# A planner for cross-attention and RWKV: spread values as one transfer, contexts as 112 and 13 rows, eight transfers in flight

## The chip, the cores and the metric

The kernel runs on one core of a Trainium2 chip. The metric is the device time in microseconds of one execution. An execution is run several times; the median is taken. A profile is one separate execution, taken with the hardware profiler; its own time stands beside its span.

Engine names in the profile: PE is TensorE (PEld its weight loads), DVE is VectorE, ACT is ScalarE, POOL is GpSimd, SP is SyncE, which issues nearly all transfers here. A "q" behind an engine's name (SPq) is its instruction queue, in which waits and DMA issues stand. Transfers run on 16 DMA engines that all queues share.

## The reference

Two layers over 16 batches of 112 tokens, width 512, all in float32. The first is cross-attention to a context of 375 rows with 16 heads of 32; the second is an RWKV block whose recurrent state has 32 heads of 16 by 16.

```python
# layer 0
a = _layer_norm(audio_kv, ln_gamma, ln_beta)          # (16, 375, 512)
Q = (x @ Wq.T) ; K = (a @ Wk.T) ; V = (a @ Wv.T)      # 16 heads of 32
attn = softmax(Q K^T * scale)
x = x + tanh(gate) * ((attn @ V) @ Wo.T)
# layer 1
xa = _ln(x, ln1_w, ln1_b)
sx = previous token of xa - xa                        # the first one from the context
xk, xw, xv, xr, xg = xa + sx * (maa_stack + tanh((xa + sx * maa_x) @ maa_w1) @ maa_w2)
w = exp(-exp(time_decay + tanh(xw @ td_w1) @ td_w2))
r, k, v, g = xr @ Wr.T, xk @ Wk.T, xv @ Wv.T, silu(xg @ Wg.T)
def step(s, rkvw):                                    # 112 steps, 32 heads
    a = k_t[..., :, None] * v_t[..., None, :]
    out = einsum('bhi,bhij->bhj', r_t, u * a + s)
    s = a + w_t[..., :, None] * s
x1 = x + (group_norm(out) * g) @ Wo.T
xc = _ln(x1, ln2_w, ln2_b)                            # and again the token before
return x1 + sigmoid(xr2 @ Wfr.T) * (relu(xk2 @ Wfk.T) ** 2 @ Wfv.T)
```

## The kernel before

**How the work is tiled.** Tokens lie in the free dimension, features on the 128 partitions in four chunks (`NC` = 4). Two batches make a group of `N` = 224 columns (`GB` = 2), and there are eight groups (`NG` = 8). The attention runs batch by batch; the second layer runs group by group in four lanes: `front` (layer norm and mixing), `begin` and `middle` (projections and scans), `back` (gate, output projection, channel mixing). Group g's `middle` runs beside the attention of later batches.

**The scan.** The state of a head is 16 by 16. For one chunk of 128 key features (8 heads of 16, `HC` = 8, `NS` = 16) and one value column index there is one recurrence over time per partition. A step n (0 to 15 in each group; chunk c = n // 4, e = n % 4) handles four value columns q at once, in a tile `kv` of 128 x 4 x 224. For this the values, which lie one feature per partition, have to be spread: each of 8 rows goes to the 16 partitions of its head. That is done through DRAM. `values(cc)` (L1212) projects the values of two chunks and copies them from PSUM to `chk_v`; `receptances(cc)` (L1218) projects the receptances and stores `chk_v` to the DRAM tile `dram_vd` (L1222) as one transfer of 128 rows. `spread(n)` (L1261) reads `dram_vd` back into `chk_kv`, in four transfers, one for each q, each of 8 rows of 223 values, each row repeated over 16 partitions, shifted by one token (`kvs[n][:, q, 1:N]`).

Then `products(n)` (L1274) multiplies `kv` by the keys in two halves (q 0 and 1 on VectorE, q 2 and 3 on GpSimd) and writes the first column of each batch from the initial state `chk_s` (ScalarE, or GpSimd for n < 2). `scans(n)` (L1290) runs two scans on VectorE, `st = w * st + kv`, and multiplies each by the receptances on GpSimd. `summed(n)` (L1310) sums over the 16 key rows by matmuls with a constant (`keep_td1c`) on TensorE. `chk_kv` and `chk_st` have three buffers each, `chk_v` has one, `dram_vd` two.

**The contexts.** `load_context(b)` (L645) loads a batch's context, 375 rows as three blocks of 125, into `ctxp_ctx` (one buffer) with one transfer of 125 partitions x 3 x 512 values (768,000 bytes); for the first batch the block is cut into 112 and 13 rows (`T` = 112) already. `normalise(b)` (L741) takes its statistics on VectorE, TensorE transposes it (`keep_ident`), and keys and values are projected from `ctxp_aT`. The buffer is free again after the transposes.

**Weights** of the other projections are loaded in slabs of 128 x 1024 values (512 KB) into five buffers `slabs_slab`; each projection of 16 matmuls reads one slab, so that a slab load waits until TensorE has done with the slab five loads before.

**What sets the order.** The kernel body does not run on the chip directly: a `Recorder` takes down all operations with their tiles, and a `Planner` (L378) simulates them with durations for each operation (`_cost`, L263; `_transfer`, L308) and writes out the order of every engine's queue; `emit` (L561) then issues the instructions in that order, which is why nearly every line of the profile is L586. On the chip, each queue runs strictly in its order, and waits are those that the data and buffers need. In `plan` (L433) the unit that can start first is chosen, and among those of the same start the one whose `place` (its due time) is earliest. For a transfer the planner counts 430 ns of issue, the bytes' time on 16 engines and 1750 ns to land. Between operations it sees dependencies by tile; DRAM tiles count as a whole (`View.meets`, L99), so that two writes to the same DRAM tile stand one after the other in the plan.

On the chip a transfer issued by SP signals on one of eight semaphores in turn, so that a transfer waits until the eighth one before it has landed.

Of the kernel before, what the change touches and what calls it, by code (L numbers as in the profile page):

```python
# [8 lines left out]
F32 = mybir.dt.float32  # L9
# [246 lines left out]
SEM = 60.0  # L256
DRAIN, REFILL, PE_LATENCY, DMA_LATENCY = 93.0, 104.0, 165.0, 1750.0
TABLE_LOAD = 1283.0
OVERLAP = {"scalar": 105.0, "vector": 85.0, "gpsimd": 0.0}
SAME_MODE = 3.0  # L260


def _cost(op):  # L263
    n = op.writes[0].size if op.writes else 1
    psum = any(v.tile.tag.space == PSUM for v in op.reads + op.writes)
    call = op.call
    if op.engine == "vector":
        if call == "tensor_tensor_scan":
            return 55 + 2.28 * n
        if call == "tensor_tensor_reduce":  # L270
            return 60 + 1.5 * n
        if call in ("bn_stats", "tensor_reduce"):
            return 50 + 1.22 * op.reads[0].size if call == "bn_stats" else 50 + 1.9 * op.reads[0].size
        if call == "bn_aggr":
            return 170
        if call == "memset":
            return 62
        if psum:
            return 140 + 1.07 * n
        if call == "tensor_tensor":  # L280
            return 200 + 0.9 * n if n < 200 or n > 700 else 150 + 1.75 * n
        if call == "scalar_tensor_tensor":
            return 200 + 1.5 * n
        return 150 + 0.96 * n
    if op.engine == "scalar":
        t = 160 + 0.84 * n
        if isinstance(op.kwargs.get("scale"), View):
            t += 110
        if isinstance(op.kwargs.get("bias"), View):
            t += 70  # L290
        if "accum_out" in op.kwargs:
            t += 190
        return t
    if call == "tensor_tensor":
        return 880 if ALU.pow in op.args else 90 + 2.57 * n
    return 190 + 0.85 * n


PACKETS = {375: 42, 892: 45, 896: 48, 1024: 52, 2048: 101, 4096: 217, 8192: 430, 512: 35}
# [8 lines left out]
def _transfer(op):  # L308
    view = (op.writes or op.reads)[0]
    if view.tile.whole and op.reads:  # L310
        view = op.reads[0]
    size = 1 if view.tile.tag.dtype == U8 else 4
    total = (view.hi - view.lo) * view.size * size
    piece = min(_run(view.index) * size, 8192)
    if op.args[0] is not view and not isinstance(op.args[0], View):
        piece = min(piece, 896)
    packet = PACKETS.get(piece, 30 + piece * 0.05)
    return total / piece * packet / 16


def _mode(op):
# [56 lines left out]
class Planner:  # L378
# [54 lines left out]
    def plan(self):  # L433
        self.array = Array()
        self.clock = {e: 0.0 for e in ("tensor", "vector", "scalar", "gpsimd", "sync")}
        self.dma, self.table = 0.0, None
        for tag in self.recorder.tags.values():
            tag.slots = [Slot() for _ in range(min(tag.bufs, len(tag.tiles)))]
            tag.strict = tag.name not in self.LOOSE
            for tile in tag.tiles:  # L440
                tile.left, tile.last = len(tile.ops), 0.0
        waiting = {e: [] for e in self.clock}
        for u in self.all:
            u.ready = 0.0
            if not u.waiting:
                waiting[u.engine].append(u)
        todo = len(self.all)
        while todo:
            best = None
            for engine, units in waiting.items():  # L450
                pick = self.choose(engine, units)
                if pick and (best is None or pick[0] < best[0]):
                    best = pick
            if best is None:
                raise RuntimeError("the plan is stuck: " + self.stuck(waiting))
            start, unit = best
            waiting[unit.engine].remove(unit)
            self.commit(unit, start)
            for user in unit.users:
                user.waiting -= 1  # L460
                if user.waiting == 0:
                    waiting[user.engine].append(user)
            todo -= 1
# [22 lines left out]
    def choose(self, engine, units):  # L486
        found, first = [], 1e18
        for u in units:
            t = self.ready(u)
            if t is None:  # L490
                continue
            if engine == "tensor":
                start = self.array.start(u, t)
            else:
                start = max(t, self.clock[engine])
            found.append((start, u))
            first = min(first, start)
        if not found:
            return None
        best = None  # L500
        for start, u in found:
            if start > first + (DRAIN + 1 if engine == "tensor" else 0.5):
                continue
            key = self.place_of(u)
            if engine == "tensor" and u.mode == self.array.mode:
                key -= SAME_MODE
            if engine == "scalar" and self.load(u):
                key += SAME_MODE
            if best is None or (key, u.number) < best[0]:
                best = ((key, u.number), start, u)  # L510
        return best[1], best[2]
# [12 lines left out]
    def commit(self, unit, start):  # L524
        for tile in unit.holds:
            if tile.slot is None:
                tag = tile.tag
                tile.slot = self.slot(tile)
                tile.slot.tile = tile
                tag.next += 1  # L530
        engine = unit.engine
        if engine == "tensor":
            ends = self.array.run(unit, start)
            issued = self.array.end
        elif unit.ops[0].call == "dma_start":
            issued = start + 430
            begin = max(issued, self.dma)
            self.dma = begin + _transfer(unit.ops[0])
            ends = [self.dma + DMA_LATENCY]
        else:  # L540
            table = self.load(unit) if engine == "scalar" else None
            if table:
                unit.table = self.table = table
                start += TABLE_LOAD
            cost = _cost(unit.ops[0])
            ends = [start + cost]
            issued = start + max(cost - OVERLAP[engine], 45.0)
        unit.start, unit.end = start, max(ends)
        self.clock[engine] = issued
        for op, end in zip(unit.ops, ends):  # L550
            for tile in {id(v.tile): v.tile for v in op.reads + op.writes}.values():
                tile.left -= 1
                tile.last = max(tile.last, end + SEM)
                if tile.left == 0:
                    tile.slot.free_at, tile.slot.tile = tile.last, None
        for user in unit.users:
            t = issued if user.engine == engine and unit.ops[0].call != "dma_start" else unit.end + SEM
            user.ready = max(user.ready, t)
        self.order.append(unit)
# [29 lines left out]
def planned(ins, out):  # L589
# [55 lines left out]
    def load_context(b, after=None):  # L645
        raw = ctxp.tile([SC, NSC, D], F32, tag="ctx", name=f"ctx_{b}")
        rows = ins["ctx"][b].rearrange("(c p) d -> p c d", p=SC)
        if b == 0:

            for c in range(NSC):  # L650
                nc.sync.dma_start(raw[:T, c, :], rows[:T, c, :])
            nc.sync.dma_start(raw[T:, :, :], rows[T:, :, :])
            return raw
        load = nc.sync.dma_start(raw, rows)
        return raw

    def load_x(g):
# [543 lines left out]
    def parts_of(g):  # L1201
# [10 lines left out]
        def values(cc):  # L1212
            vals[cc] = duo("v", f"v_{g}_{cc}", bufs=1)
            ps = project("wv1", cc, xm[2], f"pv1_{g}_{cc}")
            nc.scalar.copy(vals[cc], ps)
            vds[cc] = dram.tile([P, 2, N], F32, tag="vd", name=f"vd_{g}_{cc}")

        def receptances(cc):  # L1218
            rs[cc] = duo("r", f"r_{g}_{cc}")
            ps = project("wr1", cc, xm[3], f"pr1_{g}_{cc}")  # L1220
            copied = nc.scalar.copy(rs[cc], ps)
            nc.sync.dma_start(vds[cc], vals[cc])  # L1222
            owns[cc] = duo("own", f"own_{g}_{cc}")
            for e in range(2):
                nc.vector.scalar_tensor_tensor(
# [35 lines left out]
        def spread(n):  # L1261

            c, e = divmod(n, NQ)
            rows = vds[c // 2][:, c % 2, :].rearrange("(q e h) t -> e h q t", q=NQ, e=NQ)[e]
            kvs[n] = chk.tile([P, NQ, N], F32, tag="kv", name=f"kv_{g}_{n}", bufs=3)
            for q in range(NQ):
                load = nc.sync.dma_start(
                    kvs[n][:, q, 1:N],  # L1270
                    rows[:, q, 0 : N - 1].unsqueeze(1).broadcast_to([HC, NS, N - 1]),
                )

        def products(n):  # L1274

# [311 lines left out]
```

## Time and profile before

| | us |
|---|---|
| median of 3 runs | 1458.59 (1455.35 to 1465.3) |
| profiled execution | 1455.53 |
| its span | 1453.8 |
| mean granted TensorE clock | 0.946 |

Transfers that the change touches, as issued by SP in the profiled execution:

| transfer | count | KB each |
|---|---|---|
| `chk_kv<-dram_vd` (spread) | 512 | 111.5 |
| `dram_vd<-chk_v` (store) | 16 | 224 |
| `ctxp_ctx<-in_ctx`, whole batch | 15 | 750 |

Issuing one spread transfer takes SP 574 ns (median). VectorE waited 84.5 us in all for spreads to land, GpSimd 203.6 us, ScalarE 196.1 us. How to read the page: the busy shares are averages over stages that differ, so what a stage is limited by is read from windows of time. Idle time of an engine is put down to what ended it. The granted clock is TensorE's, 1.0 being full speed; it falls to 0.5 for some microseconds at some places. The "chain that ended last" is followed back from the last instruction to what released each step.

### The profile page before, as it was taken

To read this page: it belongs to the slowest core of one execution; us is meant where nothing else is said; L and a number is where in the kernel's file an instruction comes from. 1 tells how busy PE (TensorE), PEld (TensorE's weight loads), DVE (VectorE), ACT (ScalarE), POOL (GpSimd) and SP (SyncE) were. 2 spreads that over 40 slices of the span, in tenths; PEclk is the share of its full clock that TensorE was granted. 3 is DMA by queue.
4 is the path that set the end of the run, shared out by engine and by line. 5 is a ranking of instruction groups with operands and counts; after the bars stand their busy time and mean duration, and the time that the engine had idled before them with its cause. 6 is when DMAs were issued, how large, how long until landed. Compare 5 with 4: busy or idle time off the path is not lost.

```text
span 1453.8 us, 23511 instructions
## 1 busy us (share of the span) xinstructions
PE 1327.5 (91%) x8484; PEld 988.1 (68%) x8484; DVE 917.6 (63%) x1743; ACT 590.7 (41%) x1480; POOL 654.6 (45%) x644
## 2 busy tenths in 40 slices
PE   8999999989989999899998999989999998878867
PEld 5656686567965679556885669747696576846646
DVE  3434647874469544794547964588448858786842
ACT  2444523453144531555235532455315535423322
POOL 3001225742447324671337633374246725595740
PEclk9999999899999999899998999989999999979868
DMA  9301035221743127421473206622174225526521
GB/s 318 114 23 52 24 116 188 80 81 39 239 155 94 53 71 256 127 74 52 125 235 111 80 30 200 205 91 83 36 240 134 82 64 184 167 92 202 157 93 50
DMA packets 115532, 174.96 MB, mean 120 GB/s; under 512 B 9864, under 2 KB 87560, under 8 KB 115160
## 3 DMA queue, kind: packets, MB, share of 16 engines
q1 hardware_dynamic: 114776, 172.83, 36.4%
q8 instruction: 67, 1.10, 0.3%
q10 hardware_dynamic: 576, 0.52, 0.1%
q14 instruction: 49, 0.40, 0.1%
q0 software_dynamic: 64, 0.10, 0.0%
HBM read 164.52 MB, written 8.91 MB: 119 GB/s over the span
## 4 chain that ended last, share of the span: by engine, by line
PE 53%; DMA 18%; DVE 12%; ACT 8%; issue 4%; SPq 3%; POOL 2%; DVEq 0%; ACTq 0%; POOLq 0%
PE ps_bank L586 53%; DMA chk_kv<-dram_vd 7%; DVE chk_st L586 4%; DMA ctxp_ctx<-in_ctx 4%; SPq L586 3%; ACT hp_pr L586 3%; DMA slabs_slab<-in_wq 3%; DVE big_x L586 2%; DMA dram_vd<-chk_v 2%; DMA slabs_slab<-in_wfr 1%; DVE chk_kv L586 1%; DVE hp_pr L586 1%; ACT tmp_tmp L586 1%; POOL chk_st L586 1%; DMA slabs_slab<-in_wg 1%
## 5 line engine op out<-in xcount | busy, mean ns | idle before, releaser
L586 POOL TENSOR_TENSOR chk_st<-chk_st,chk_r 128x448 f32<-128x448 f32 x256 | 307.2, 1222 | 168.6 <-DVE chk_st L586 156.3
L586 DVE TENSOR_TENSOR_SCAN chk_st<-ps_w_w,chk_kv 128x448 f32<-128x448 f32 x256 | 263.4, 1069 | 12.2 <-ACT ps_w_w L586 7.6
L586 POOL TENSOR_TENSOR chk_kv<-chk_kv,chk_k 128x444 f32<-128x444 f32 x128 | 155.2, 1216 | 210.2 <-DMA chk_kv<-dram_vd 203.6
L586 PE MATMUL ps_bank<-big_x,slabs_slab 128*128 128x224 f32 x1024 | 214.8, 368 | 3.1 <-DMA slabs_slab<-in_wg 2.8
L586 PEld LDWEIGHTS ps_bank<-big_x,slabs_slab 128*128 128x128 f32 x1024 | 203.1, 200 | 13.3 <-issue 6.2
L586 PE MATMUL ps_bank<-ctxp_aT,keep_wk 128*128 128x375 f32 x512 | 183.4, 507 | 3.2 <-ACT hp_prT L586 3.1
L586 DVE TENSOR_TENSOR chk_kv<-chk_kv,chk_k 128x444 f32<-128x444 f32 x128 | 125.9, 988 | 84.6 <-DMA chk_kv<-dram_vd 84.5
L586 PE MATMUL ps_bank<-keep_wv,ctxp_aT 128*125 128x512 f32 x384 | 168.6, 592 | 0.0
L586 ACT ACTIVATE hp_pr<-hp_pr,sm_mn 112x375 f32<-112x375 f32 x256 | 152.4, 598 | 31.1 <-DVE sm_mn L586 31.1
L586 DVE CUSTOM_DVE_ANT_0 hp_pr<-ps_bank,hp_mb 112x375 f32<-112x375 f32 x256 | 124.5, 541 | 43.0 <-PE ps_bank L586 41.2
L586 PEld LDWEIGHTS ps_bank<-ctxp_aT,keep_wk 128*128 128x128 f32 x512 | 99.3, 200 | 68.9 <-issue 10.6
L586 PE MATMUL ps_bank<-keep_ident,hp_pr 112*125 112x112 f32 x768 | 115.4, 298 | 27.7 <-ACT kvp_oR L586 20.0
L586 PEld LDWEIGHTS ps_bank<-keep_ident,hp_pr 112*125 112x125 f32 x768 | 100.5, 202 | 56.4 <-ACT kvp_oR L586 27.1
L586 PEld LDWEIGHTS ps_bank<-keep_wv,ctxp_aT 128*125 128x125 f32 x384 | 71.9, 188 | 85.9 <-issue 83.4
L586 ACT COPY chk_kv<-chk_s 128x8 f32<-128x8 f32 x112 | 22.8, 204 | 230.5 <-DMA chk_kv<-dram_vd 196.1
L586 POOL TENSOR_TENSOR big_x<-big_x,big_xa 128x448 f32<-128x448 f32 x48 | 59.9, 1267 | 76.6 <-DVE big_x L586 76.2
L586 PE MATMUL ps_bank<-chk_st,keep_td1c 128*32 128x224 f32 x1024 | 77.3, 381 | 17.7 <-POOL chk_st L586 17.5
L586 ACT COPY hp_prT<-ps_bank 125x448 f32<-125x448 f32 x112 | 57.4, 531 | 70.1 <-PE ps_bank L586 69.7
L586 PE MATMUL ps_bank<-kvp_kT,kvp_qT 32*112 32x375 f32 x512 | 68.3, 518 | 4.1 <-DVE sm_mn L586 2.6
L586 DVE SCALAR_TENSOR_TENSOR big_x<-ps_bank,keep_vecs,big_sx 128x224 f32<-128x224 f32 x160 | 59.4, 439 | 14.2 <-PE ps_bank L586 14.2
L586 PEld LDWEIGHTS ps_bank<-chk_st,keep_td1c 128*32 128x32 f32 x1024 | 29.8, 113 | 51.2 <-POOL chk_st L586 33.0
L586 PE MATMUL ps_bank<-big_o,slabs_slab 128*128 128x224 f32 x256 | 59.6, 393 | 4.5 <-POOL big_o L586 4.2
(130 smaller groups left out, 1981.1 us busy)
## 6 DMA issues: line engine op xcount, KB each, us to landing
chk_kv<-dram_vd SPq DMA_DIRECT2D x512, 111.5 KB
slabs_slab<-in_wo SPq DMA_DIRECT2D x32, 512.0 KB
ctxp_ctx<-in_ctx SPq DMA_DIRECT2D x15, 750.0 KB
slabs_slab<-dram_wv1c SPq DMA_DIRECT2D x16, 512.0 KB
slabs_slab<-in_wk SPq DMA_DIRECT2D x16, 512.0 KB
slabs_slab<-in_wr SPq DMA_DIRECT2D x16, 512.0 KB
slabs_slab<-in_wg SPq DMA_DIRECT2D x16, 512.0 KB
slabs_slab<-in_wfk SPq DMA_DIRECT2D x16, 512.0 KB
```

The lines of the kernel that those rows point to most:

```text
L586: call(*[real(a) for a in op.args], **{k: real(v) for k, v in op.kwargs.items()})
```

## The change

It has four parts, in one diff.

1. **Spread.** `dram_vd` is laid out as (2 chunks, 32 rows, 4 q, 224), so that the four q of a row are neighbours in DRAM. A spread is one transfer of 8 rows x 895 contiguous values, each row repeated over 16 partitions. The values that land in the first column of a q (from the end of the q before) are overwritten by the initial state, as the first column always was.
2. **Store.** To bring the values into that layout, the store becomes four transfers of 32 partitions x 2 x 224, and stands in `values` instead of `receptances`.
3. **Contexts** of the batches 1 to 15 are loaded as two transfers, of 112 and of 13 rows.
4. **Planner.** An issue counts 500 ns; a transfer starts only when the eighth one before it has landed (`FLIGHTS`); its own time is spread over as many engines as the largest divisor up to 16 of its rows, and the queue after it over 16. Several engines' durations are changed.

SP issues 440 instructions' groups in a new order (376 before, where equal neighbours are counted as one). TensorE, VectorE, ScalarE and GpSimd get the same operations in another order.

```diff
+ISSUE, FLIGHTS = 500.0, 8
...
         if call == "tensor_tensor_reduce":
-            return 60 + 1.5 * n
+            return 25 + 1.58 * n
...
+        if call == "reciprocal":
+            return 250
         if psum:
-            return 140 + 1.07 * n
+            return (200 if call == "scalar_tensor_tensor" else 140) + 1.07 * n
...
         if call == "scalar_tensor_tensor":
-            return 200 + 1.5 * n
+            return 150 + 1.35 * n
...
-        t = 160 + 0.84 * n
+        t = 175 + 0.82 * n
...
         if "accum_out" in op.kwargs:
-            t += 190
+            t += 80
...
-        return 880 if ALU.pow in op.args else 90 + 2.57 * n
-    return 190 + 0.85 * n
+        return 880 if ALU.pow in op.args else 90 + 2.5 * n
+    return 200 + 0.85 * n
...
-    packet = PACKETS.get(piece, 30 + piece * 0.05)
-    return total / piece * packet / 16
+    packet = PACKETS.get(piece, 25 + piece * 0.05)
+    rows = view.hi - view.lo if not view.tile.whole else 128
+    engines = max(d for d in range(1, 17) if rows % d == 0)
+    busy = total / piece * packet
+    return busy / engines, busy / 16
...
                 start = max(t, self.clock[engine])
+                if u.ops[0].call == "dma_start":
+                    start = max(start, self.flights[-FLIGHTS])
...
-            issued = start + 430
+            issued = start + ISSUE
             begin = max(issued, self.dma)
-            self.dma = begin + _transfer(unit.ops[0])
-            ends = [self.dma + DMA_LATENCY]
+            alone, shared = _transfer(unit.ops[0])
+            self.dma = begin + shared
+            ends = [begin + alone + DMA_LATENCY]
+            self.flights.append(ends[0] + SEM)
...
-        load = nc.sync.dma_start(raw, rows)
+        nc.sync.dma_start(raw[:T], rows[:T])
+        nc.sync.dma_start(raw[T:], rows[T:])
         return raw
...
-            vds[cc] = dram.tile([P, 2, N], F32, tag="vd", name=f"vd_{g}_{cc}")
+            vds[cc] = dram.tile([2, NQ * HC, NQ, N], F32, tag="vd", name=f"vd_{g}_{cc}")
+            for q in range(NQ):
+                nc.sync.dma_start(
+                    vds[cc][:, :, q, :].rearrange("c r t -> r c t"),
+                    vals[cc][32 * q : 32 * q + 32],
+                )
...
             copied = nc.scalar.copy(rs[cc], ps)
-            nc.sync.dma_start(vds[cc], vals[cc])
...
-            rows = vds[c // 2][:, c % 2, :].rearrange("(q e h) t -> e h q t", q=NQ, e=NQ)[e]
+            rows = vds[c // 2][c % 2, HC * e : HC * e + HC].rearrange("h q t -> h (q t)")
             kvs[n] = chk.tile([P, NQ, N], F32, tag="kv", name=f"kv_{g}_{n}", bufs=3)
-            for q in range(NQ):
-                load = nc.sync.dma_start(
-                    kvs[n][:, q, 1:N],
-                    rows[:, q, 0 : N - 1].unsqueeze(1).broadcast_to([HC, NS, N - 1]),
-                )
+            nc.sync.dma_start(
+                flat(kvs[n])[:, 1:],
+                rows[:, : NQ * N - 1].unsqueeze(1).broadcast_to([HC, NS, NQ * N - 1]),
+            )
```

More of the change, by code (lines that the diff above doesn't have):

```diff
@@ L435, in plan @@
         self.clock = {e: 0.0 for e in ("tensor", "vector", "scalar", "gpsimd", "sync")}
-        self.dma, self.table = 0.0, None
+        self.dma, self.table, self.flights = 0.0, None, [0.0] * FLIGHTS
         for tag in self.recorder.tags.values():
```

## The prediction

> **What bounds the kernel now.** I read the busy shares first, then the chain that ended last, then the windows of 40 us, then the chain inside one window. The page opens with
>
> ```profile
> span 1453.8 us, 23511 instructions
> ...
> PE 1327.5 (91%) x8484; PEld 988.1 (68%) x8484; DVE 917.6 (63%) x1743; ACT 590.7 (41%) x1480; POOL 654.6 (45%) x644
> ...
> PE 53%; DMA 18%; DVE 12%; ACT 8%; issue 4%; SPq 3%; POOL 2%; DVEq 0%; ACTq 0%; POOLq 0%
> ```
>
> TensorE is busy 1327.5 of 1453.8 us and the change removes no matmul. So what can be won is its idle time (126 us) and the time in which it ran at a low clock. DMA holds 18% of the chain, so I asked where. Windows of four stages (columns: length, busy us of PE, PEld, DVE, ACT, POOL, granted clock, DMA share, GB/s):
>
> ```profile
> 600.00:640.00 40.00, 34.13 (x203) 19.88 (x203) 35.87 (x61) 19.41 (x56) 30.37 (x28) 0.87 0.28 86
> 720.00:760.00 40.00, 40.00 (x253) 36.51 (x252) 21.97 (x38) 10.32 (x32) 16.34 (x15) 1.00 0.77 252
> ```
>
> A dense stage (720 to 760) with TensorE at 40.00 of 40 hides every transfer. A shared stage (600 to 640), in which the scans run beside the attention, has TensorE at 34.13 and the clock at 0.87; 240, 400, 760 and 920 show 0.87 too. The chain inside it:
>
> ```profile
> 588.09 9.33 DMA ctxp_ctx<-in_ctx
> 597.42 0.02 issue
> 597.44 4.89 DMA chk_kv<-dram_vd
> 602.33 0.02 issue
> 602.35 0.04 ACTq L586
> 602.39 0.04 issue
> 602.43 0.20 ACT chk_kv L586
> 602.63 2.37 ACT hp_pr L586 x8
> ```
>
> The context load takes 9.33 us to land. SP cannot issue the eighth transfer after it (597.44) until it has landed; that transfer belongs to a spread, whose landing VectorE, GpSimd and ScalarE wait for in order, with the softmax rows queued behind them. TensorE sees it last (timeline, idle time in brackets):
>
> ```profile
> 599.75 2.28 PE L586 MATMUL ps_bank<-kvp_kT,kvp_qT 32*112 32x375 f32 x8 [0.78 <-DVE sm_mn L586]
> 605.18 1.18 PE L586 MATMUL ps_bank<-keep_ident,hp_pr 112*125 112x112 f32 x4 [3.15 <-ACT kvp_oR L586]
> ```
>
> Why so long? Windows in which a context load runs alone, and in which spreads run alone:
>
> ```profile
> 76.00:79.00 3.00, 3.00 (x19) 2.24 (x18) 2.51 (x10) 2.68 (x10) 0.83 (x3) 1.00 0.33 128
> 615.90:618.20 2.30, 2.29 (x18) 1.47 (x19) 1.52 (x7) 1.14 (x3) 2.12 (x3) 1.00 0.50 160
> ```
>
> The context runs on a third of the 16 DMA engines (five, at 128/5 = 25.6 GB/s each), a spread on half. 768,000 bytes at 128 GB/s are 6.0 of the 9.33 us.
>
> **The change part by part**, against the profiled execution (1455.53 us, 1.7 outside the span; the median of the runs is 3.1 higher).
>
> *Context as 112 and 13 rows.* If the 112 rows use all 16 engines at 25.6 GB/s, 688,128 bytes take 1.7 us; the 13 rows (79,872 bytes) add 0.2 on thirteen engines, 3.1 on one. So data take 1.9 to 4.8 us instead of 6.0; I take 1.9, because the slabs of 128 rows bring the window 720 to 760 to 252 GB/s, twice what five engines carry, and only the load of 125 rows shows a third. The load lands 4.1 us earlier, about 5.2 after its issue. The stall of 3.5 us of VectorE (line below) is shorter than that and goes.
>
> ```profile
> 598.61 0.62 DVE L586 TENSOR_TENSOR chk_kv<-chk_kv,chk_k 128x444 f32<-128x444 f32 x1 [3.52 <-DMA chk_kv<-dram_vd]
> ```
>
> Five shared stages have it (TensorE idle 3.0 near 252, 3.1 at 428, 3.9 at 599 and 602, 4.0 at 773 and 776, 3.6 at 946: 17.6 us), each followed by some 10 us at half clock (the windows of 2 us show 0.50 from 604 to 612). Of these TensorE was busy 7.6, so half of it, 3.8 us, was lost: 19 in five. Ceiling 36.6. Floor 14: VectorE's own idle there (0.7, 3.4, 3.5, 3.6, 3.1), if VectorE, busy 35.87 of 40, binds. I take 25. What is late next is VectorE.
>
> The Trainium skill ("DMA: Bandwidth & Descriptors", section on why a DMA increments its semaphore by 16) says a DMA runs on the largest number up to 16 that divides the slowest dimension of both sides: 125 gives 5, 112 gives 16, 13 gives 13, a spread's 8 source rows give 8. The two windows agree for 5 and 8. The same page ("Rules for kernel authors") advises against splitting into partition halves, since both use the same engines anyway; by that rule this part is worth nothing and the sum would be 1460. The trace's third of the engines speaks for the first rule here.
>
> *Attention alone.* At 74 and 113 us VectorE waits for the same load (3.58 us idle before its statistics at 82.42), TensorE is idle 2.85 and 2.30 us, and 3.4 us at half clock follow the first (1.7 lost). Ceiling 6.9, floor 2 if the statistics then bind; I take 5.
>
> *Spread as one transfer.* 512 issues of 0.574 us become 128: SP is free of 220 us, mostly under waits for PE. Four transfers of 16 packets per engine, issued from 614.47, moved their data from 615.7 to 619.0. One transfer of 895 values still has 8 source rows, so I keep 8 engines: 458,240 bytes at 8 x 25.6 GB/s are 2.2 us after the 1.25 us of start-up, 3.5 in all. The whole is there 1 us earlier; the first half, which VectorE needs first, 0.8 us later (before: two transfers, 2.75). Dense stages hide both. In the last 150 us, where nothing does, VectorE waits four times for spreads (2.4, 1.1, 2.0, 3.9: 9.4 us); bounds 9 gained, 3 lost (4 x 0.8). I take 3 gained. Each spread also takes one of the eight places in flight instead of four.
>
> *Stores.* One store becomes four, and the order of the changed program puts a slab load between each two: store, wfk, store, wfr, store, wq, store, wfr, then three spreads; before, store, wfk, three spreads. Slab loads wait for TensorE to free a slab, 3.0 us each in a dense stage (16 matmuls in 3.19). So the first spread is issued three slabs, 9 us, later. The cover is the dense stage: before, scans 0 to 2 end at 555.84 and the next starts at 582.27, since their three buffers wait for TensorE's sums at 580.6. That is 26 us, so 9 cost nothing in groups 1 to 5. In the last group it is gone:
>
> ```profile
> 1308.81 4.23 DMA dram_vd<-chk_v
> ...
> 1313.74 2.79 DMA chk_kv<-dram_vd
> ```
>
> There the fourth store stands behind a load into the slab that the receptances have just used. It costs at most 9 per uncovered group; groups 0, 6 and 7 make 27, and 0 if the spreads' gain and TensorE's other work cover it. I take 6 for the last group and 1 each for the two others: 8.
>
> *The planner* places everything anew (TensorE has the same 1962 rows in another order; its changes between tiling modes, counted in the order, go from 375 to 369, table loads from 39 to 37, 1.3 us each). No row prices an order. The idle time of TensorE not named above is 126 - 23 = 103 us; I allow a ninth of it either way, 12, and take 0, since nothing in the order decides its sign.
>
> Sum: -25 - 5 - 3 + 8 = -25, so 1455.5 - 25 = 1430.
>
> **The rivals.**
> *The stores bind (slower).* Four stores behind waits for slabs start every group's scans 9 us later. It decides where the first spread lands after TensorE reaches the group's first sums, so if the new order moves those 17 us forward. For: the chain carries the store in groups 0, 2, 4, 5, 6 and 7. Against: the 26 us of cover. If all eight groups pay, 8 x 9 = 72, less 33 gained: 1495; with five paying, 1468.
> *VectorE takes the stall over (no change).* The shared stage has VectorE at 35.87 of 40. Then the contexts give the floor, 14 + 2, the spreads nothing, and the stores cost 8: 1448. For: the tail of each group alternates between VectorE, GpSimd and TensorE. Against: the 3.5 us are VectorE's own idle time.
> *The split does not use the engines.* If 112 rows stayed on five engines, the 13 would queue behind: nothing gained but the spreads and places in flight, and 8 lost: 1460.
>
> **How the numbers follow.** About 1% is what a measurement here can tell from no change (the runs spread over 0.7%): below 1444 is faster, above 1473 slower. Forecast (1403 to 1444): 0.66. VectorE binds, or the split does nothing (1444 to 1466): 0.20. Stores bind (1466 to 1495): 0.14. The forecast's low end is both ceilings of the contexts and 9 from the spreads, 1455.5 - 36.6 - 6.9 - 9 = 1403; a better order on top is the little left out below. The upper end takes in the second and third rival and leaves out the first. Forecast's own range: 1403 to 1444.
>
> **What would show it.** Right: context loads landing in about 5 us; windows like 600 to 640 at a clock near 1.00 with TensorE above 37; no DMA share near 0.33 alone; spreads of one transfer with data for 2.2 us at a DMA share of 0.50. Stores: scans 0 to 2 end near 565 in a dense stage, TensorE still at 40 of 40. Wrong: TensorE waiting for chk_st at the start of each shared stage (the stores), an idle VectorE on chk_kv of the old size (the spread), or clocks still at 0.87 with VectorE at 38 of 40 (VectorE binds).

## The result and the profile after

| | before | after |
|---|---|---|
| median, us | 1456.97 (4 runs) | 1509.80 (4 runs, 1492.92 to 1515.21) |
| profiled execution, span | 1455.53, 1453.8 | 1492.92, 1491.1 |
| TensorE busy in it | 1327.5 | 1328.6 |

The ratio is 1.0334, 95% interval 1.0241 to 1.0427: slower, where 1430 was forecast. Medians are over all executions of a run; the ratios, and the differences that are said to go by them, leave out the few executions that took longer at a lower granted clock. The profiled execution is the fastest of the four, so its page shows 37 of the 53 us. TensorE's busy time in it is unchanged, so its idle time grew from 126 to 163 us. The page's first lines and its chain that ended last:

```profile
span 1491.1 us, 22649 instructions
...
PE 1328.6 (89%) x8484; PEld 978.1 (66%) x8484; DVE 920.0 (62%) x1743; ACT 593.4 (40%) x1478; POOL 667.6 (45%) x644
...
PE 52%; DMA 23%; DVE 11%; ACT 5%; issue 4%; POOL 4%; SPq 1%; ACTq 0%; DVEq 0%; POOLq 0%
```

DMA's share went from 18 to 23%, and of it the spread alone is 19% (7% before). The waits say who pays (total us, times, longest):

```profile
ACT chk_kv L596 <- DMA chk_kv<-dram_vd: 300.5, 91, 8.6
...
DVE chk_kv L596 <- DMA chk_kv<-dram_vd: 163.6, 56, 10.5
POOL chk_kv L596 <- DMA chk_kv<-dram_vd: 163.1, 69, 21.0
```

VectorE's wait for spreads has doubled (84.5 before), ScalarE's has grown by half (196.1), GpSimd's has fallen (203.6). TensorE waits longer for what comes after the spreads, the scans' products, and for slabs. The row of the scans' products before, then the same row and the largest slab row after:

```profile
PE ps_bank L586 <- POOL chk_st L586: 17.5, 14, 5.3
```

```profile
PE ps_bank L596 <- POOL chk_st L596: 33.1, 22, 5.9
...
PE ps_bank L596 <- DMA slabs_slab<-in_wg: 12.1, 3, 6.2
```

The three slab rows (`wq`, `wg`, `wfv`) add up to 24.1 us, 9.2 before; with the scans' products that is about 30 of the 37 us of new idle time. The chain in two stretches, one with a context load and one with spreads:

```profile
809.56 5.03 DMA ctxp_ctx<-in_ctx
```

```profile
591.79 7.19 DMA chk_kv<-dram_vd
...
607.60 5.81 DMA chk_kv<-dram_vd
```

The context part did what was forecast: 9.33 us from issue to landing became 5.03. The spreads did not: 3.5 us was forecast, and the chain has 7.19 and 5.81. Three windows of 40 us (columns as in the prediction):

```profile
560.00:600.00 40.00, 33.94 (x249) 26.27 (x249) 25.15 (x50) 15.06 (x45) 19.15 (x16) 0.91 0.67 205
600.00:640.00 40.00, 38.13 (x241) 23.21 (x240) 35.13 (x59) 18.93 (x54) 33.34 (x32) 1.00 0.37 97
720.00:760.00 40.00, 34.91 (x208) 30.56 (x207) 18.24 (x32) 6.81 (x20) 17.91 (x16) 0.93 0.69 207
```

The first of these windows before:

```profile
560.00:600.00 40.00, 39.14 (x310) 31.72 (x309) 19.90 (x40) 15.26 (x43) 12.44 (x12) 1.00 0.63 208
```

The stage from 600 is better than it was (TensorE 38.13 against 34.13, clock 1.00 against 0.87). It is the end of the dense stages, where TensorE had been at 40.00 or 39.14, that now has idle TensorE. The chain there (start, length, what), SP's timeline ahead of it and TensorE's at its end (idle time in brackets):

```profile
551.87 13.26 PE ps_bank L596 x70
565.12 0.02 issue
565.14 11.33 DMA slabs_slab<-in_wg
```

```profile
560.92 2.54 SPq L596 DMA_DIRECT2D chk_kv<-dram_vd  x2
563.55 0.41 SPq L596 DMA_DIRECT2D slabs_slab<-in_wo  x1
```

```profile
576.60 3.65 PE L596 MATMUL ps_bank<-big_x,slabs_slab 128*128 128x224 f32 x9 [5.44 <-DMA slabs_slab<-in_wg]
```

SP issues two spreads when VectorE's scans free their buffers (560.86 and 562.82), the slab loads `wo` and `wg` follow them, and these spreads end their data only at 567.2 and 571.8. The slab that TensorE needs at 571.16 lands 11.33 us after its issue. While the two spreads move, about 30 packets of slabs start in a us; from 572 to 574, behind them, it is 85 and 102. The scans of these spreads begin only near 590, so here the spread is not late for its own reader but in the way of another's load.

### The profile page after: what moved, and what is told of

Its sections match the earlier page's. It is cut to its first block, busy times and chain, and to the rows that moved or that the text cites. A ratio compares the mean times of both kernels' runs of the same rounds, so it can differ in the third digit from the quotient of the medians.

```text
span 1491.1 us, 22649 instructions
## 1 busy us (share of the span) xinstructions
PE 1328.6 (89%) x8484; PEld 978.1 (66%) x8484; DVE 920.0 (62%) x1743; ACT 593.4 (40%) x1478; POOL 667.6 (45%) x644
## 4 chain that ended last, share of the span: by engine, by line
PE 52%; DMA 23%; DVE 11%; ACT 5%; issue 4%; POOL 4%; SPq 1%; ACTq 0%; DVEq 0%; POOLq 0%
PE ps_bank L596 52%; DMA chk_kv<-dram_vd 19%; DVE chk_st L596 4%; ACT hp_pr L596 2%; POOL chk_st L596 2%; DMA slabs_slab<-in_wg 2%; DVE chk_kv L596 1%; DVE hp_pr L596 1%; DMA dram_vd<-chk_v 1%; ACT big_xa L596 1%; ACT tmp_tmp L596 1%; POOL chk_kv L596 1%; DMA slabs_slab<-in_wq 1%; DVE big_mk L596 1%; DVE big_xa L596 1%
## 5 line engine op out<-in xcount | busy, mean ns | idle before, releaser
L596 POOL TENSOR_TENSOR chk_kv<-chk_kv,chk_k 128x444 f32<-128x444 f32 x128 | 166.1, 1298 | 193.2 <-DMA chk_kv<-dram_vd 163.1
L596 DVE TENSOR_TENSOR chk_kv<-chk_kv,chk_k 128x444 f32<-128x444 f32 x128 | 132.5, 1035 | 163.8 <-DMA chk_kv<-dram_vd 163.6
L596 PE MATMUL ps_bank<-big_x,slabs_slab 128*128 128x224 f32 x1024 | 208.8, 360 | 15.2 <-DMA slabs_slab<-in_wg 12.1
L596 PEld LDWEIGHTS ps_bank<-big_x,slabs_slab 128*128 128x128 f32 x1024 | 197.1, 194 | 24.9 <-issue 16.8
L596 PE MATMUL ps_bank<-keep_ident,hp_pr 112*125 112x112 f32 x768 | 110.0, 287 | 21.3 <-DVE sm_mn L596 6.6
L596 PEld LDWEIGHTS ps_bank<-keep_wv,ctxp_aT 128*125 128x125 f32 x384 | 71.8, 188 | 84.5 <-issue 82.2
L596 PEld LDWEIGHTS ps_bank<-keep_ident,hp_pr 112*125 112x125 f32 x768 | 93.8, 192 | 47.1 <-DVE sm_mn L596 10.5
L596 PE MATMUL ps_bank<-chk_st,keep_td1c 128*32 128x224 f32 x1024 | 90.0, 397 | 38.0 <-POOL chk_st L596 33.1
L596 POOL TENSOR_TENSOR big_kk<-big_kk 128x448 f32<-128x448 f32 (+1 forms) x28 | 26.1, 932 | 148.7 <-ACT big_kk L596 148.1
L596 PE MATMUL ps_bank<-kvp_kT,kvp_qT 32*112 32x375 f32 x512 | 73.6, 547 | 2.5 <-DVE big_mk L596 2.1
L596 PE MATMUL ps_bank<-hp_prT,kvp_v 125*32 125x112 f32 x1536 | 52.1, 270 | 23.1 <-DVE big_mk L596 7.6
```

The source lines that it names most:

```text
L596: call(*[real(a) for a in op.args], **{k: real(v) for k, v in op.kwargs.items()})
```

## The experiments

Times are medians; ratios are to the kernel before, run on the same chip, with 95% intervals. "Before's order" means that the plan was made from the old operations, so that every engine's queue keeps the order it had, and only the transfers named differ when they are issued.

**1. The parts one by one.**

`ctx_only`, before's order:

```diff
-        load = nc.sync.dma_start(raw, rows)
+        nc.sync.dma_start(raw[:T], rows[:T])
+        nc.sync.dma_start(raw[T:], rows[T:])
```

> The kernel before, every queue in its old order, only the fifteen context loads issued as 112 and 13 rows. Theory (the context term of the prediction holds, -25 in shared stages and -5 in the attention alone): about 1430, 1415 to 1445, contexts landing near 5 us. Rival (VectorE takes the stall over): 1441 to 1455. Rival (the split does not reach 16 engines): 1457, landing still above 8 us.

1427.3 us, ratio 0.9761 (0.9718 to 0.9804). From the issue of a context load to its last packet, the median is 4.5 us against 8.0 before. The theory held. The rivals' 1441 to 1455 (VectorE takes the stall over) and 1457 (the split does nothing) did not. The group that takes the context's statistics, before and then in `ctx_only` (busy, mean ns, idle before it):

```profile
L586 DVE BATCH_NORM_STATS2 sm_st<-ctxp_ctx 125x6 f32<-125x512 f32 x48 | 32.2, 671 | 29.3 <-DMA ctxp_ctx<-in_ctx 29.3
```

```profile
L590 DVE BATCH_NORM_STATS2 sm_st<-ctxp_ctx 125x6 f32<-125x512 f32 x48 | 32.1, 669 | 9.8 <-DMA ctxp_ctx<-in_ctx 9.8
```

`spread_store_only`, before's order:

```diff
-            nc.sync.dma_start(vds[cc], vals[cc])
+            for q in range(NQ):
+                nc.sync.dma_start(
+                    vds[cc][:, :, q, :].rearrange("c r t -> r c t"),
+                    vals[cc][32 * q : 32 * q + 32],
+                )
...
-            for q in range(NQ):
-                load = nc.sync.dma_start(
-                    kvs[n][:, q, 1:N],
-                    rows[:, q, 0 : N - 1].unsqueeze(1).broadcast_to([HC, NS, N - 1]),
-                )
+            nc.sync.dma_start(
+                flat(kvs[n])[:, 1:],
+                rows[:, : NQ * N - 1].unsqueeze(1).broadcast_to([HC, NS, NQ * N - 1]),
+            )
```

> The kernel before, every queue in its old order, with one transfer of 895 values in the place of the fourth of each spread's four, and the store as four transfers back to back at its old place. Theory (one transfer is slower than four: data for 3.6 us where I had assumed 2.2, landing 5.0 us after its issue, its first half 2 us later than before): 1470 to 1500, VectorE's wait for chk_kv above 110 us against 84.5. Rival (the loss is in the planner's new order, and the transfers as such cost nothing): 1445 to 1462.

1538.95 us, ratio 1.0522 (1.0469 to 1.0574): 76 us lost by the ratio, 80 by the medians, more than expected. Its profiled execution took 1566.7 us, above the median, so no wait is read from it, only when transfers landed.

`planner_only`: all of the diff in `_cost`, `_transfer` and `plan`, and no transfer changed.

> The kernel before with the planner's changes alone (500 ns an issue, eight in flight, transfers by engines, the new durations); every transfer as before, the order of all queues new. Theory (the transfers are the loss): 1457 with an allowance of 12 either way, as the prediction put it. Rival (the new order is the loss): 1480 to 1510.

1421.01 us, ratio 0.9717 (0.9677 to 0.9757): 38 us won, outside both expectations. The new order is far from being the loss.

`after_four`: the changed kernel, but

```diff
...
-            nc.sync.dma_start(
-                flat(kvs[n])[:, 1:],
-                rows[:, : NQ * N - 1].unsqueeze(1).broadcast_to([HC, NS, NQ * N - 1]),
-            )
+            for q in range(NQ):
+                nc.sync.dma_start(
+                    kvs[n][:, q, 1:N],
+                    rows[:, q, 0 : N - 1].unsqueeze(1).broadcast_to([HC, NS, N - 1]),
+                )
```

> The changed kernel with each spread as four transfers of 223 values again, read from the new layout (stores in four, contexts split, planner new, order planned anew). Theory (one transfer is the loss): 1435 to 1465, VectorE's wait for chk_kv back under 100 us from 163.6. Rival (the four stores or the planner are the loss): 1490 to 1515.

1433.13 us, ratio 0.9799 (0.9755 to 0.9843), just under the theory's window. Putting this one part back turns 1510 into 1433. VectorE's wait for spreads is 94.8 us.

`store_only`, before's order: new layout and four stores, spreads as four transfers.

> The kernel before, every queue in its old order, new layout of the DRAM tile and the store as four transfers back to back at its old place; spreads still four transfers of 223 values. It splits the 80 us that spread_store_only lost. Theory (the single large transfer is the loss): 1455 to 1468, VectorE's wait for chk_kv about 85 us. Rival (four stores, each with one of the eight places in flight, are a good part of it): 1480 or more.

1453.46 us, ratio 0.9976 (0.9942 to 1.0010): the four stores back to back cost nothing in this order. So the loss of `spread_store_only` is the spread's, against the 3 that the prediction gave as a gain.

`plan_ctx`: contexts and planner, with the spread and the store of before.

> The changed kernel without its spread and store (contexts split, planner new, spread as four transfers and the store as one, as before). Theory (context and planner each gain what they gained alone, and partly the same stalls): 1390 to 1415, below both kernels and below planner_only's 1421. Rival (they remove the same stalls): 1418 to 1425.

1408.50 us, ratio 0.9624 (0.9558 to 0.9689), as the theory had it and below both kernels. The two gains (32 and 38) share about 20 us.

**2. Why is one transfer slower than four?** Three candidates: its packets are slow; both halves land together, and it is issued later; or the planner believes in an earlier landing.

`after_halves`: the changed kernel, with

```diff
+            for at in (0, 2 * N):
+                nc.sync.dma_start(
+                    flat(kvs[n])[:, at + 1 : at + 2 * N],
+                    rows[:, at : at + 2 * N - 1].unsqueeze(1).broadcast_to([HC, NS, 2 * N - 1]),
+                )
```

> The changed kernel with each spread as two transfers of 447 contiguous values. VectorE's half of a step then has its own landing. Theory (what costs is that the first half waits for the whole, and that 3580-byte packets run slowly): about halfway, 1450 to 1480, first half landing near 3.3 us after its issue. Rival (the price lies in the size of the packet alone, not in the common landing): 1490 to 1510. Rival (only the common landing matters): 1430 to 1445.

1445.05 us, ratio 0.9895 (0.9847 to 0.9944): most of the loss gone. That is just under the theory's window and at the upper edge of the second rival's (only the common landing matters, 1430 to 1445), so this run does not part the two; the first rival, the size of the packet alone, is out. The first half ends 3.15 us after its issue (median).

`after_price`: the changed kernel with a spread counted as 8 rows in `_transfer`.

```diff
     rows = view.hi - view.lo if not view.tile.whole else 128
+    if op.reads and op.reads[0].tile.whole and op.reads[0].tile.tag.name.endswith("vd"):
+        rows = HC
```

> The changed kernel with one line more in the planner: a spread counts 8 rows, so 3.3 us of data instead of 1.6; on the chip the same transfers in another order. Theory (the late landing itself is what is paid, by VectorE with its three buffers): 1490 to 1515. Rival (the loss comes from the planner's belief that a spread lands 3.9 us after SP begins to issue it, so that SP stands at spreads with slab loads behind): 1430 to 1470.

1477.50 us, ratio 1.0121 (1.0072 to 1.0169): between the two expectations. `_transfer` takes the rows from the SBUF side, 128, so it counts 16 engines for a spread that has 8 source rows. With the true number, some 30 of the 77 us between `after_four` and the changed kernel come back. It is one new order, and orders alone differ here by as much as 25 us for no cause that was found (see `plan_ctx` and `after_four`), so that the belief itself is worth these 30 is likely, not shown.

`four_late`, before's order: the four transfers of a spread in another sequence.

```diff
-            for q in range(NQ):
+            for q in (2, 3, 0, 1):
```

> The kernel before, every queue in its old order; only the four transfers of a spread change places: q 2, 3, 0, 1 in the place of 0, 1, 2, 3. The first to be issued now writes the half of the buffer that the second scan reads, so that all four wait for the second scan; sizes, packets and count are those of before. In spread_store_only one transfer was issued 0.07 us after the second scan's end and landed 5.2 after it (median), where the four of before were issued from 0.92 before it and landed 2.0 (first half) and 3.7 after. Theory (the early issue of the first half is most of what was lost): first half near 4.4, so (4.4 - 2.0)/(5.2 - 2.0) of the 80 us: 1500 to 1530. Rival (the size of the packets, 3.6 us of data for 2.2, is what was lost): 1455 to 1470.

1487.51 us, ratio 1.0176 (1.0125 to 1.0226): between theory and rival, below the theory's 1500. Issuing behind the second scan costs, but about 26 us, not the 76 that one transfer lost. The run changes two things at once: all four are issued later, and VectorE's half is now the last to land.

`after_padded`: the changed kernel with rows of 2048 values in the DRAM tile.

```diff
-            vds[cc] = dram.tile([2, NQ * HC, NQ, N], F32, tag="vd", name=f"vd_{g}_{cc}")
+            vds[cc] = dram.tile([2, NQ * HC, 2048], F32, tag="vd", name=f"vd_{g}_{cc}")
...
```

> The changed kernel with the rows of the DRAM tile 8192 bytes apart instead of 3584. It asks why 128 packets of 3580 bytes on 8 engines take 3.6 us instead of the 2.2 that their shortest duration (140 ns, 16 to an engine) would make. If the rows' nearness in DRAM is the cause: data near 2.3 us, median packet 140, and 1470 to 1490. If not: data 3.6 us and 1500 to 1515.

1496.58 us, ratio 1.0228 (1.0182 to 1.0274), data for 3.3 us when alone (3.6 in the changed kernel), median packet 187 ns (182). This lies between the two expectations, far nearer to the second. The rows' nearness in DRAM is not the main cause; the ratio's interval meets that of the changed kernel only at its edge, so some us may lie there.

`after_stores_together`: the changed kernel, the store planned as one operation and issued as four.

> The changed kernel with the store planned as one operation and issued as four transfers back to back, so that no slab loads stand between them. Theory (the 25 us between plan_ctx, 1408, and after_four, 1433, are the slab loads between the stores): 1478 to 1492. Rival (that difference is the other order alone): 1500 to 1515.

1505.72 us, ratio 1.0274 (1.0213 to 1.0334): no difference from the changed kernel that can be measured, so the rival held. The slab loads between the stores do not cost here. What the 25 us between `plan_ctx` and `after_four` are is left open.

`after_sixteen`: the same, but every row of values lies in DRAM twice.

```diff
-            vds[cc] = dram.tile([2, NQ * HC, NQ, N], F32, tag="vd", name=f"vd_{g}_{cc}")
+            vds[cc] = dram.tile([2, NQ * HC, 2, NQ, N], F32, tag="vd", name=f"vd_{g}_{cc}")
...
-            rows = vds[c // 2][c % 2, HC * e : HC * e + HC].rearrange("h q t -> h (q t)")
+            rows = vds[c // 2][c % 2, HC * e : HC * e + HC].rearrange("h d q t -> (h d) (q t)")
...
-                rows[:, : NQ * N - 1].unsqueeze(1).broadcast_to([HC, NS, NQ * N - 1]),
+                rows[:, : NQ * N - 1].unsqueeze(1).broadcast_to([2 * HC, NS // 2, NQ * N - 1]),
```

> As after_stores_together, but every row of values is stored twice (eight transfers of 56 KB), so that a spread reads 16 rows, each to 8 partitions, instead of 8 rows, each to 16. If the number of source rows sets the number of engines, a spread's data take half the time, 1.2 to 1.8 us, and lands 1.8 to 2.4 us earlier: 1435 to 1465. If the engines are not the limit: data 3.6 us, and the time of after_stores_together or some us above it.

1403.82 us, ratio 0.9607 (0.9564 to 0.9650). TensorE's, VectorE's, ScalarE's and GpSimd's queues are in the same order as in `after_stores_together`, SP has eight stores for four: about 100 us (98 by the ratios) come from the number of source rows, and the time is 30 to 60 us below what was expected, though the whole lands 2.1 us earlier, as expected. The plan, which counts 16 engines for a spread, is now also right. Windows in which a spread moves its data with no other load, of the changed kernel and then of `after_sixteen` (the last two columns are DMA share and GB/s):

```profile
615.90:619.30 3.40, 3.40 (x11) 1.74 (x10) 3.37 (x5) 2.04 (x6) 3.40 (x5) 1.00 0.41 128
```

```profile
257.60:259.50 1.90, 1.90 (x8) 0.94 (x8) 1.86 (x4) 1.01 (x3) 1.21 (x2) 1.00 0.79 236
```

The same bytes take 3.4 us at a share of 0.41, or 1.9 at 0.79. The Trainium skill ("DMA: Bandwidth & Descriptors", section on why a DMA increments its semaphore by 16) gives the number of engines as the largest up to 16 that divides the slowest dimension of both sides; shares under 0.5 and near 0.8 agree with 8 and 16. The chain and the wait of `after_stores_together`, then of `after_sixteen`:

```profile
PE 50%; DMA 25%; DVE 13%; ACT 5%; issue 3%; POOL 3%; SPq 1%; ACTq 0%; DVEq 0%; POOLq 0%
```

```profile
DVE chk_kv L600 <- DMA chk_kv<-dram_vd: 167.2, 67, 7.2
```

```profile
PE 68%; DVE 14%; DMA 6%; ACT 5%; issue 4%; POOL 4%; SPq 0%; ACTq 0%; DVEq 0%; POOLq 0%
```

```profile
DVE chk_kv L600 <- DMA chk_kv<-dram_vd: 59.3, 24, 4.5
```

DMA leaves the chain, 25 to 6%, and TensorE carries 68% of it.

**3. What was still open.**

`sixteen_old_order`: `spread_store_only` with every row twice.

> spread_store_only (before's order on every queue, one transfer a spread) with every row of values stored twice, so that the spread reads 16 rows. Issued after the second scan, as there, and still one landing for both halves. Theory (what costs is how late the transfer lands, and that is set by eight engines): 1450 to 1475, from 1539. Rival (the later issue and the common landing cost by themselves): 1500 to 1530.

1447.09 us, ratio 0.9915 (0.9878 to 0.9952), from 1538.95, just under the theory's window. One transfer, issued late, with a common landing, is then no worse than four.

`flights_only` and `durations_only` split `planner_only`.

> The kernel before with the planner's view of transfers alone (500 ns, eight in flight, engines by rows), the old durations of the engines. It splits the 38 us of planner_only (1421). If the waits of SP that the plan did not know are the gain: 1415 to 1430. If the durations are: 1450 to 1462.

> The kernel before with the planner's new durations of VectorE, ScalarE and GpSimd alone. The other half of that split: 1450 to 1462 if the transfers' model is the gain, 1415 to 1430 if the durations are. Both near 1435 would say that any new order differs by this much.

1437.37 us, ratio 0.9864 (0.9795 to 0.9933), and 1462.32 us, ratio 1.0050 (1.0007 to 1.0092). The view of transfers alone won 20 us, the durations alone lost 5; together they won 38. The sum is not additive, and which wait was removed was not found.

`sixteen_halves`: `after_sixteen` with two transfers of 447 values.

> after_sixteen (1404) with each spread as two transfers of 447 values, 16 rows each. The first half is issued after the first scan and should land 1.5 us before the second scan's end plus 3, that is about 1.6 after it against 3.6. If landing earlier still pays: 1385 to 1398. If the spreads are hidden by now: 1400 to 1410.

1373.43 us, ratio 0.9416 (0.9356 to 0.9477): 84 us below before and the fastest of all, beyond what was expected. Its first line and its chain:

```profile
span 1372.3 us, 23133 instructions
...
PE 68%; DVE 17%; ACT 5%; DMA 4%; issue 4%; POOL 2%; SPq 0%; DVEq 0%; ACTq 0%; POOLq 0%
```

**The landing and the time.** Worked out from the traces' packets over steps 5 to 15 of every group, as medians in us after the end of the second scan of three steps earlier, which frees the whole buffer. The halves are those of q 0 and 1 (VectorE's) and q 2 and 3 (GpSimd's); the earlier one is VectorE's except in `four_late`. The time is the median without the long executions; the landings of `spread_store_only` are from its profiled execution, a long one.

| kernel | first issue | earlier half | whole | time |
|---|---|---|---|---|
| before | -0.92 | 2.0 | 3.7 | 1457 |
| `four_late` (q 2, 3 first) | 0.06 | 3.1 | 4.9 | 1488 |
| `spread_store_only` | 0.07 | | 5.2 | 1535 |
| `sixteen_old_order` | 0.07 | | 3.4 | 1447 |
| `after_four` | -0.92 | 2.0 | 4.1 | 1433 |
| `after_halves` | -0.95 | 2.2 | 4.0 | 1445 |
| after | 0.07 | | 5.4 | 1510 |
| `after_padded` | 0.07 | | 5.1 | 1497 |
| `after_stores_together` | 0.07 | | 5.7 | 1503 |
| `after_sixteen` | 0.07 | | 3.6 | 1404 |
| `sixteen_halves` | -0.92 | 1.7 | 2.8 | 1373 |

The first four rows have before's order, the others a plan with the contexts split, nearly each with an order of its own. In each set, time roughly follows the landing of the whole, but not in proportion: from `four_late` to `spread_store_only` the whole lands 0.3 us later and the kernel loses 50 us more (by the ratios), while GpSimd's half lands 2.1 us later. Which of the two halves costs most was not tried alone. Before's trace also shows where it begins to count. From the freeing of the buffer until VectorE has nothing left ahead of the step's products, 7.3 us pass in the median, but under 5.2 us in 25 of those 88 steps and under 3.8 in only 3. A whole that lands at 3.7 is covered almost everywhere, and one at 5.2 in seven of ten steps at best. In the changed kernel a quarter of the steps lands after 6.6 (6.1 before).

## Why the prediction was wrong

**Contexts: right in size.** The term was -25 and -5; `ctx_only` measured -32. Landing near 5 us, the clock near 1.00 from 600 to 640 and TensorE above 37 there were seen in the changed kernel as predicted. The way there was another than the ceiling's 17.6 us of idle time and 19 of clock: in the profile of `ctx_only` TensorE's busy time fell by 28.8 us (1327.5 to 1298.7, granted clock 0.946 to 0.966), its idle time by 6.8. The rule of sixteen engines, weighed at 4.1 us of earlier landing, held (3.5 measured, 8.0 to 4.5). The Trainium skill's advice ("DMA: Bandwidth & Descriptors", "Rules for kernel authors") not to split into partition halves, by which this part would be worth nothing, does not fit a load of 125 rows here: its ground is that both halves use all 16 engines, and the whole load showed a share of 0.33.

**Spread: the step that failed.** The prediction took 8 engines at 25.6 GB/s, a rate read from the context load's packets of 2048 bytes, so 2.2 us of data, a landing 3.5 us after the issue, and a gain of 3. Alone, the data take 3.6 us and the last packet ends 5.0 after the issue: packets of 3580 bytes took 203 ns in the mean, 17.7 GB/s for each engine, where 140 ns was the shortest common duration. The window of spreads that the prediction itself showed has 160 GB/s on eight engines, 20 each; taken from that row, the data would have been 2.9 us and the landing 4.1. Nor is one transfer quicker than four: alone, the four of before took 3.1 us for their data and 4.5 from the first issue to the last packet (medians), so one is 0.5 us slower, where the prediction had it 1 us faster.

Two things were missed besides the size. First, "issued from 614.47" is 0.95 us before the end of the second scan at 615.42: the transfers of q 0 and 1 wait only for the first scan. One transfer waits for both. So against the freeing of the buffer the whole went from 3.7 to 5.2 us and VectorE's half from 2.0 to 5.2, not "1 us earlier" and "0.8 us later"; of the whole's 1.5 us, 1.0 is the later issue and about 0.5 the slower data. Second, the cover: "Dense stages hide both", and the rest was priced at four waits in the last 150 us. The shared stages lie between, where a quarter of the steps leave less than 5.2 us. The worst that the prediction allowed for was 3 lost; with before's order it was +80 by the ratios (`spread_store_only` against `store_only`), with the new planner, in an order of its own, +77 (the changed kernel against `after_four`).

`after_sixteen` and `sixteen_old_order` show that a single transfer, issued late, costs nothing when it is quick enough; `after_halves`, that on eight engines an early first half takes back 65 of the 77 us, in an order of its own. Either remedy takes back most or all, so the loss is that of a single transfer on eight engines, not of one of the two alone. `four_late` puts the later issue, with VectorE's half last, at about 26 us; `after_price` suggests that about 30 of the 77 are the plan's belief in sixteen engines for a spread, a part of the change that the prediction did not read.

**Stores: no cost in before's order, open in the new one.** The scans 0 to 2 end at 562.82 in the third group (565 was forecast), and the cover held there: 520 to 560 has TensorE at 40.00 of 40. `store_only` and `after_stores_together` put the stores, and the slabs between them, at nothing, against +8. With the new planner `after_four`, which differs from `plan_ctx` by layout, stores and the order that follows, is 25 us slower, and the cause is open. The sign that the prediction gave for the stores, TensorE waiting for `chk_st`, was seen (17.5 us before, 33.1 after), but with the same stores and four transfers a spread it is 18.8 (`after_four`): it is the spread's. The rival that the stores bind had the right sign with the wrong mechanism: the stall for slabs at 571 stands behind spreads, not stores. The rival that VectorE takes the contexts' stall over fell with `ctx_only`, and so did that of an idle split.

**Planner: sign and size missed.** 0, with 12 either way, was -38. The argument that no row prices an order was true, and the allowance, a ninth of the idle time not named elsewhere, had no row behind it.

The sum as measured: contexts and planner -51 together, spread and store with the order that follows from them +101 (`plan_ctx` 1408.5 to 1509.8), so +50, where the forecast had -30, 0 and +5.

## What to carry to other kernels

Joining small transfers into one can make them land later: the joined transfer is issued only when its whole buffer is free, and its first part lands with its last. Read both the rate for its own packet size and the moment its buffer comes free from the trace. Here the joined transfer lost on eight engines and not on sixteen; no run shows that joining itself gains, since four transfers with sixteen source rows were not tried. Compare the landing with the time until the consumer is ready, step by step, since a quarter of the steps had little slack here, and look at whose loads share the engines meanwhile. Where a source is a few rows repeated over many partitions, storing the rows twice can double the engines, and two halves keep the early issue: here 1373 us against 1457.

## What the runs showed of the hardware

Packets of 892 bytes took 41 ns (median, 21.8 GB/s on an engine), 1788 bytes 74 ns (24.2, `after_halves`), but 3580 bytes 182 ns in the changed kernel and 208 in `after_sixteen`, although 140 occurs often and would be 25.6 GB/s. By the means, which set how long a transfer's data take, the sizes differ less: 44 ns (20.3 GB/s), 90 (19.8) and 203 (17.7). With 8 and with 16 engines the packets are about equally slow while the sum goes from 128 to 236 GB/s, so it is no common rate that they share; with rows 8192 bytes apart they stay at 187. What slows them is open; other destinations and other alignments were not tried. The Trainium skill ("DMA: Bandwidth & Descriptors", "Rules for kernel authors") recommends to coalesce many small transfers; here four of 112 KB joined to one cost 5.5% on eight engines (1.0522 against 0.9976), and nothing with 16 source rows (0.9915).
